# Layer 3's products in four tiles of 32 array columns

## The chip, the cores and the metric

One core of a Trainium2 chip runs the whole program. The metric is device time in microseconds for one execution; the median over runs is quoted. All runs below are of the fast state. Where two kernels are compared, the ratio is the mean time of one kernel's fast runs over the mean of the other's in the same rounds, so it is not quite the ratio of the medians quoted beside it.

## The reference, cut to what matters

Four graph-attention layers run over 16 batches of 1024 nodes with 256 features, in float32. The change touches layer 3, with 4 heads of 64 features:

```python
h = jnp.einsum('bnd,hde->bhne', nodes_embed, W)          # H = 4 heads, 64 features each
...
weight = jnp.where(node_adj[:, None] == 0, NEG, weight)
attention = jax.nn.softmax(weight, axis=-1)
dst = jnp.einsum('bhij,bhje->bhie', attention, h) + bias[None, :, None, :]
```

The kernel does not form the softmax. It makes unnormalized weights, and for each head multiplies them by 64 value columns and by one column whose product is the row's total. It divides afterwards.

## The kernel before

Two streams, one with the even batches and one with the odd, are traced side by side. Each generator yields its own cost in estimated microseconds, and `LAG` sets how far the second stream trails. A build-time scheduler then orders each engine's instructions. `tc.keep_in_program_order(x)`, called a pin below, adds one constraint: x comes after the instruction traced just before it on its engine. It does not forbid others in between.

VectorE makes a weight tile of 128 sources x 1024 destinations:

```python
for j in range(NI):                       # NI = 8 source blocks
    w = edges.tile([P, N], F32, name=f"weights{b % 2}")
    nc.vector.scalar_tensor_tensor(w, r, c(j), masks[b][:, j // 2, :, j % 2], op0=op, op1=ALU.mult)
    into.append(w)
    ...
    yield 0.5
```

Layer 3 then goes by head `h` and half `g` of the destinations:

```python
LAG = 120.0
...
for n in range(H * NH):                   # 4 heads x 2 halves
    h, g = divmod(n, NH)
    if g == NH - 1:
        behind = weigh3(h + 1)            # the next head's weights
        yield from start(behind, b)
    accT = accumulator(b)[: E + 1, :]     # 65 rows of one PSUM bank
    for j in range(NI):
        ...
        nc.tensor.matmul(accT, V3[:, j, h, :], weights[h * NI + j][:, ts(g, HALF)],
                         start=(j == 0), stop=(j == NI - 1))
        if n > 0:
            next(behind, None)
        yield 0.9
    ...
    sums = wide.tile([E + 1, HALF], F32, name="sums")
    nc.scalar.copy(sums, accT)
    next(coming, None)                    # a step of loading the batch after next
    ...
    for i in range(NG):
        nc.tensor.transpose(acc[:, i, :], sums[:, ts(i, P)], ident[: E + 1, : E + 1])
    inverse(inv, acc[:, :, E])
    nc.vector.tensor_mul(...)
```

The other layers' products are `nc.tensor.matmul(accs[i], weights[j][:, ts(i, P)], V[:, j, : D + 1], ...)`: 128 stationary columns (the operand that a weight load puts into TensorE's array first), 257 moving ones (streamed past it).

## Time and profile before

| | before |
|---|---|
| time, median of 4 runs | 3115.68 us (3114.26 to 3117.85) |
| span of the profiled run | 3112.0 us |
| TensorE busy | 2981.7 us (96%) |
| VectorE busy | 2337.8 us (75%) |
| layer-3 matmuls | 2048, of 65 stationary and 512 moving columns |

The page gives busy time by engine, then the chain of work that ended last, then groups of instructions by source line: output <- inputs, sizes, count | busy us, mean ns of one | idle time before and who ended it. The prediction below shows the lines that matter. A matmul's duration includes a tail that its neighbours hide, and the profile models a matmul's end rather than seeing it, so its price is read from the distance between starts, in the chain in order of time.

### The profile page before, as it was taken

How to read it: one execution, taken by the hardware profiler on the slowest of the kernel's cores; microseconds unless marked ns; L12 is line 12 of the kernel's file. 1: busy time of each engine (PE TensorE's matmuls, PEld its weight loads, DVE VectorE, ACT ScalarE, POOL GpSimd, SP SyncE). 2: the span in 40 equal slices, each digit the busy share in tenths (PEclk: the TensorE clock that was granted, in tenths of full speed). 3: DMA queues.
4: the chain of work that ended last, by engine and by line, in shares of the span. 5: the costliest groups of instructions: out<-in, count | busy, mean ns of one | idle time of the engine just before them, and what ended most of it. 6: DMA issues, size and time to landing. Idle time of an engine off the chain costs nothing.

```text
span 3112.0 us, 35525 instructions
## 1 busy us (share of the span) xinstructions
PE 2981.7 (96%) x12678; PEld 2047.5 (66%) x12678; DVE 2337.8 (75%) x5234; ACT 737.1 (24%) x1729; POOL 1081.2 (35%) x1405
## 2 busy tenths in 40 slices
PE   7899999999999999999999999999999999999986
PEld 5676756767566675766757667575666767667652
DVE  6678787777877768787786877778777787777856
ACT  1221312223131231312213122231322313122130
POOL 2323433244242333424244242342423434243332
PEclk9999999999999999999999999999999999999998
DMA  8112212022121122111122120221212222001010
GB/s 126 28 28 41 41 14 54 14 41 41 28 44 19 33 41 41 35 20 48 21 41 41 14 54 14 41 41 28 45 15 37 41 35 41 7 28 27 1 28 15
DMA packets 116872, 105.52 MB, mean 34 GB/s; under 512 B 73681, under 2 KB 91217, under 8 KB 116689
## 3 DMA queue, kind: packets, MB, share of 16 engines
q0 software_dynamic: 44256, 81.80, 16.2%
q1 hardware_dynamic: 72432, 21.37, 3.5%
q8 instruction: 103, 1.69, 0.2%
q14 instruction: 81, 0.66, 0.1%
HBM read 153.49 MB, written 33.55 MB: 60 GB/s over the span
## 4 chain that ended last, share of the span: by engine, by line
PE 78%; DVE 15%; POOL 3%; ACT 2%; issue 1%; DMA 1%; SPq 0%; ACTq 0%; POOLq 0%; DVEq 0%
PE acc L398 35%; PE acc L511 25%; PE acc L289 11%; DVE weights L310 8%; PE misc L282 3%; PE row L306 2%; ACT adj_i L141 1%; PE misc L526 1%; POOL y L471 1%; POOL rstd L257 1%; DVE V L355 1%; DVE stats L269 1%; POOL x_b L337 1%; DVE centered L274 1%; ACT below L333 1%
## 5 line engine op out<-in xcount | busy, mean ns | idle before, releaser
L398 PE MATMUL acc<-V,weights 128*128 128x257 f32 x6144 | 1449.3, 383 | 38.0 <-DVE weights L310 29.8
L398 PEld LDWEIGHTS acc<-V,weights 128*128 128x128 f32 x6144 | 1141.6, 190 | 348.6 <-DVE weights L310 100.6
L511 PE MATMUL acc<-weights,V 128*65 128x512 f32 x2048 | 955.9, 592 | 2.0 <-DVE weights L310 1.7
L310 DVE SCALAR_TENSOR_TENSOR weights<-row,ex,mask 128x1024 f32<-128x1024 f32 x512 | 627.8, 1274 | 6.1 <-PE row L306 5.6
L257 POOL TENSOR_TENSOR rstd<-rstd,minus_half 128x2 f32<-128x2 f32 (+1 forms) x320 | 299.5, 936 | 943.1 <-DVE rstd L256 930.7
L289 PE MATMUL acc<-W,hT 128*128 128x259 f32 (+1 forms) x2048 | 515.4, 389 | 26.0 <-ACT hT L284 14.8
L310 DVE SCALAR_TENSOR_TENSOR weights<-row,V,mask 128x1024 f32<-128x1024 f32 x384 | 482.0, 1274 | 46.6 <-PE row L306 46.6
L511 PEld LDWEIGHTS acc<-weights,V 128*65 128x65 f32 x2048 | 273.9, 138 | 361.0 <-issue 312.5
L289 PEld LDWEIGHTS acc<-W,hT 128*128 128x128 f32 x2048 | 379.2, 191 | 138.4 <-ACT hT L284 38.2
L337 POOL TENSOR_TENSOR x_b<-x_b,above 128x256 f32<-128x256 f32 x256 | 196.5, 771 | 427.5 <-DVE above L336 345.1
L333 ACT ACTIVATE below<-acc,inv 128x256 f32<-128x256 f32 x256 | 120.3, 473 | 771.4 <-DVE inv L326 623.6
L269 DVE BATCH_NORM_STATS2 stats<-x_b 128x6 f32<-128x256 f32 x512 | 207.6, 418 | 92.9 <-POOL x_b L337 83.5
L284 ACT COPY hT<-misc 128x512 f32<-128x512 f32 x256 | 146.7, 586 | 344.7 <-PE misc L282 344.6
L471 POOL TENSOR_TENSOR y<-y,bias 128x512 f32<-128x512 f32 x64 | 82.8, 1294 | 406.9 <-DVE y L529 323.5
L274 DVE TENSOR_SCALAR centered<-x_b,mv 128x256 f32<-128x256 f32 x512 | 192.6, 384 | 15.7 <-PE misc L282 12.2
L351 ACT ACTIVATE V<-acc,rstd 128x3 f32<-128x3 f32 x384 | 98.2, 262 | 418.0 <-PE acc L289 418.0
L282 PEld LDWEIGHTS misc<-ident,centered 128*128 128x128 f32 x1024 | 124.1, 141 | 109.7 <-issue 49.0
L282 PE MATMUL misc<-ident,centered 128*128 128x128 f32 x1024 | 162.7, 278 | 31.1 <-DVE centered L274 21.6
L335 DVE TENSOR_SCALAR above<-acc,inv 128x256 f32<-128x256 f32 x256 | 122.5, 481 | 84.4 <-ACT below L333 83.8
L521 ACT COPY sums<-acc 65x512 f32<-65x512 f32 x128 | 74.5, 582 | 409.6 <-PE acc L511 409.6
L355 DVE TENSOR_SCALAR V<-acc,rstd,V 128x256 f32<-128x256 f32 x256 | 133.4, 538 | 37.7 <-ACT V L351 34.9
L141 ACT ACTIVATE adj_i<-adj_i,minus_half 128x1024 bf16<-128x1024 bf16 x128 | 145.8, 1139 | 20.0 <-DMA adj_i<-in_adj_dram 20.0
(69 smaller groups left out, 1870.3 us busy)
## 6 DMA issues: line engine op xcount, KB each, us to landing
adj_i<-in_adj_dram POOLq DMA_DIRECT2D x128, 256.0 KB, 3.9
narrow<-in_adj_dram POOLq DMA_DIRECT2D x64, 256.0 KB, 9.4
out_dram<-y POOLq DMA_DIRECT2D x32, 512.0 KB, 4.3
x_b<-in_x_dram POOLq DMA_DIRECT2D x14, 1024.0 KB, 5.6
x_b<-in_x_dram SPq DMA_DIRECT2D x2, 1024.0 KB, 7.2
mask<-narrow SPq DMA_TRANSPOSE x64, 3.7
W<-in_L_gnn_W_dram SPq DMA_DIRECT2D x3, 256.0 KB, 6.1
weights<-in_L_gnn_a_dram SPq DMA_DIRECT2D x3, 256.0 KB, 7.9
```

The lines of the kernel that those rows point to most:

```text
L141: square = nc.scalar.activation(adj_i, adj_i, AF.Square, bias=minus_half, accum_out=squares[:, b, i : i + 1])
L257: nc.gpsimd.tensor_tensor(r, r, minus_half.to_broadcast([P, n]), op=ALU.pow)
L269: nc.vector.bn_stats(stats, xb[:, 2 * pair + n, :])
L274: nc.vector.tensor_scalar(centered[:, n, :], xb[:, 2 * pair + n, :], mv[:, n, 0:1], 0.0, op0=ALU.subtract, op1=ALU.max,)
L282: nc.tensor.transpose(turned[:, k, ts(n, P)], centered[:, n, ts(k, P)], ident)
L289: nc.tensor.matmul(projected, hT[:, k, ts(n, P)], W[l][:, k, :], start=(k == 0), stop=(k == NK - 1),)
L310: nc.vector.scalar_tensor_tensor(w, r, c(j), masks[b][:, j // 2, :, j % 2], op0=op, op1=ALU.mult)
L333: nc.scalar.activation(below, acc[:, :D], AF.Exp, scale=inv)
L337: nc.gpsimd.tensor_add(xi, xi, above)
L355: nc.vector.tensor_scalar(V[:, i, :D], projected[:, :D], rstd, V[:, i, D : D + 1], op0=ALU.mult, op1=ALU.mult,)
L398: nc.tensor.matmul(accs[i], weights[j][:, ts(i, P)], V[:, j, : D + 1], start=(j == 0), stop=(j == NI - 1),)
L511: nc.tensor.matmul(accT, V3[:, j, h, :], weights[h * NI + j][:, ts(g, HALF)], start=(j == 0), stop=(j == NI - 1),)
```

## The change

The intent is to fill the array. A product with 65 columns leaves about half of it empty. The changed kernel puts each product in a tile of 32 columns and issues four for four different tiles, to run side by side: two halves of the destinations x two halves of the 64 features. The totals get tiles of their own.

```diff
-    LAG = 120.0
+    LAG = 111.0
+    QUAD = P // 4
...
+        def in_tiles(parts, accT: bass.AP, first: bool, last: bool):
+            for n, (values, moving) in enumerate(parts):
+                made = nc.tensor.matmul(
+                    accT[ts(n, QUAD), :], values, moving, start=first, stop=last
+                )
+                if pinned:
+                    tc.keep_in_program_order(made)
+                pinned.append(made)
...
+        def add_values(h: int, j: int):
+            for n in (j + 1, j):
+                parts = [
+                    (V3[:, n, h, ts(e, QUAD)], moving)
+                    for moving in halves_of(h, n)
+                    for e in range(2)
+                ]
+                in_tiles(parts, acc, n == 1, n == NI - 2)
+
+        def add_totals(h: int, j: int):
+            parts = [
+                (V3[:, j + n, h, E:].to_broadcast([P, QUAD]), halves_of(h, j + n)[g])
+                for g, n in ((0, 1), (0, 0), (1, 1), (1, 0))
+            ]
+            in_tiles(parts, total, j == 0, j == NI - 2)
...
+        for h in range(H):
+            acc = accumulator(b)
+            total = accumulator(b)
+            if h == 0:
+                for j in range(0, NI, 2):
+                    next(behind)
+                    next(behind)
+                    pinned = []
+                    add_values(h, j)
+                    yield 1.8
...
+            step = 4 if h == 0 else 2
+            for first in range(0, NI, step):
+                pinned = []
+                for j in range(first, first + step, 2):
+                    add_totals(h, j)
+                    if h > 0:
+                        add_values(h, j)
+                for _ in range(step):
+                    next(behind, None)
+                yield 1.8 if h == 0 else 2.7
... (two copies of 128 x 512 a head, eight 128-column transposes, one reduction, one inverse,
     one multiply a head in place of two of half the size)
```

More of the change, by code (lines that the diff above doesn't have):

```diff
@@ L496, in weigh3, with halves_of @@
             )
+        def in_tiles(parts, accT: bass.AP, first: bool, last: bool):
[6 more added lines that the diff above has]
+                pinned.append(made)
+        def halves_of(h: int, j: int):
+            return [weights[h * NI + j][:, ts(g, HALF)] for g in range(NH)]
@@ L498, in batch @@
         behind = weigh3(0)
         yield from start(behind, b)
-        for n in range(H * NH):
-            h, g = divmod(n, NH)
-            if g == NH - 1:
-                behind = weigh3(h + 1)
-                yield from start(behind, b)
-            accT = accumulator(b)[: E + 1, :]
-            for j in range(NI):
-                if n == 0:
-                    next(behind)
-                nc.tensor.matmul(
-                    accT, V3[:, j, h, :], weights[h * NI + j][:, ts(g, HALF)],
-                    start=(j == 0), stop=(j == NI - 1),
-                )
-                if n > 0:
+        for h in range(H):
[3 more added lines that the diff above has]
+                for j in range(0, NI, 2):
+                    next(behind)
+                    next(behind)
+                    pinned = []
+                    add_values(h, j)
+                    yield 1.8
+                for _ in behind:
+                    pass
+            behind = weigh3(h + 1)
+            yield from start(behind, b)
+            step = 4 if h == 0 else 2
[6 more added lines that the diff above has]
+                for _ in range(step):
@@ L516, in batch @@
                     next(behind, None)
-                yield 0.9
+                yield 1.8 if h == 0 else 2.7
             for _ in behind:
                 pass
-            sums = wide.tile([E + 1, HALF], F32, name="sums")
-            nc.scalar.copy(sums, accT)
-            next(coming, None)
+            copies = []
+            for accT in (acc, total) if h == 0 else (total, acc):
+                copies.append(wide.tile([P, HALF], F32, name="sums"))
+                nc.scalar.copy(copies[-1], accT)
+                next(coming, None)
@@ L523, in batch @@
+            sums, totals = copies if h == 0 else copies[::-1]
             yield 0.5
-            acc = psum.tile([P, NG, E + 1], F32, name="misc")
+            turned = psum.tile([P, NG, P], F32, name="misc")
             for i in range(NG):
-                nc.tensor.transpose(acc[:, i, :], sums[:, ts(i, P)], ident[: E + 1, : E + 1])
-            inv = small.tile([P, NG], F32, name="inv4")
-            inverse(inv, acc[:, :, E])
+                nc.tensor.transpose(turned[:, i, :], totals[:, ts(i, P)], ident)
@@ L529, in batch @@
+            inv = small.tile([P, NH, NG], F32, name="inv8")
+            nc.vector.tensor_reduce(
+                inv, turned[:, :, ::QUAD].rearrange("p i (g n) -> p g i n", n=2), AX.X, ALU.add
+            )
+            inverse(inv, inv)
+            turned = psum.tile([P, NG, NH, E], F32, name="misc")
+            for i in range(NG):
+                nc.tensor.transpose(
+                    turned[:, i].rearrange("p g e -> p (g e)"), sums[:, ts(i, P)], ident
+                )
             nc.vector.tensor_mul(
-                y[:, ts(g, NG), h, :], acc[:, :, :E], inv.unsqueeze(2).to_broadcast([P, NG, E])
+                y[:, :, h, :].rearrange("p (g i) e -> p g i e", g=NH),
+                turned.rearrange("p i g e -> p g i e"),
+                inv.unsqueeze(3).to_broadcast([P, NH, NG, E]),
@@ L531, in batch @@
             )
             yield 0.5
-            if g == NH - 1:
-                if h > 0:
-                    rescale(*normed.pop())
-                normed.append(center(h))
-                yield 1.0
+            if h > 0:
+                rescale(*normed.pop())
+            normed.append(center(h))
+            yield 1.0
         for _ in coming:
```

## The prediction

> **What bounds the kernel now.** I read the page first: busy time by engine, the 40 slices, then the chain that ended last. These lines carry it:
>
> ```profile
> span 3112.0 us, 35525 instructions
> PE 2981.7 (96%) x12678; PEld 2047.5 (66%) x12678; DVE 2337.8 (75%) x5234; ACT 737.1 (24%) x1729; POOL 1081.2 (35%) x1405
> ...
> PE   7899999999999999999999999999999999999986
> ...
> PEclk9999999999999999999999999999999999999998
> ...
> PE 78%; DVE 15%; POOL 3%; ACT 2%; issue 1%; DMA 1%; SPq 0%; ACTq 0%; POOLq 0%; DVEq 0%
> ```
>
> TensorE is busy in nearly every slice at full clock and holds 78% of the chain. VectorE at 75% is second, with 15%. So a microsecond of matmul streaming removed is mostly a microsecond of the run, until VectorE's 2338 us become the floor. Next, the groups by line, for the one to be changed (layer 3's products) and those around it:
>
> ```profile
> L398 PE MATMUL acc<-V,weights 128*128 128x257 f32 x6144 | 1449.3, 383 | 38.0 <-DVE weights L310 29.8
> L511 PE MATMUL acc<-weights,V 128*65 128x512 f32 x2048 | 955.9, 592 | 2.0 <-DVE weights L310 1.7
> L511 PEld LDWEIGHTS acc<-weights,V 128*65 128x65 f32 x2048 | 273.9, 138 | 361.0 <-issue 312.5
> L521 ACT COPY sums<-acc 65x512 f32<-65x512 f32 x128 | 74.5, 582 | 409.6 <-PE acc L511 409.6
> L526 PE MATMUL misc<-ident,sums 65*128 65x65 f32 x512 | 55.9, 231 | 1.6 <-ACT sums L521 0.7
> L325 DVE TENSOR_SCALAR inv<-misc 128x4 f32<-128x4 f32 x128 | 19.4, 152 | 48.7 <-PE misc L526 48.6
> ```
>
> The program has 1024 layer-3 products (16 batches x 4 heads x 2 halves x 8 source blocks) and the trace has 2048 matmuls: each float32 product is two passes, each with its own weight load. Only 65 of 128 columns are used, while each pass streams all 512 moving columns. A duration is not the price: pipelined matmuls overlap their tails. The price is the distance between neighbours, from the timeline:
>
> ```profile
> 1539.43 0.87 PE acc L398 x4
> 1540.29 0.86 PE acc L511 x2
> 1541.15 2.60 PE acc L398 x12
> 1543.75 0.24 PE misc L526 x4
> 1543.99 0.88 PE row L306 x8
> 1544.87 2.57 PE acc L511 x6
> ```
>
> (That is the chain of waits in order of time: start, length, count.) Layer 3 costs 2.57/6 = 0.429 us a pass, 0.858 us a product. A 65-column transpose costs 0.24/4 = 0.06 us, a 128-column one 0.88/8 = 0.11 us. The two streams alternate every product or few. Layer 3 is 2048 x 0.429 = 879 us of TensorE, 28% of the span.
>
> **What the Trainium skill says.** (1) TensorEngine Tiling (Array Packing), section Key Properties: tiles can load and multiply in parallel, but changing the tiling mode drains the engine. No tiled product is in this trace, so it can neither confirm nor deny this. (2) TensorE: Matmul & The Clock Gate, section Measured speedup vs the span model: three column tiles of 32 with 512 columns gave 2.38 times, with some 4 ns more per tile. That need not be float32. (3) The same page, section The mechanism: matmuls start and end in strict program order. Under rivals I say why that matters for two passes. (4) The same page, section Single matmul latency: warm latency is (398 + N)/2.4 ns. The trace agrees if a float32 pass counts two cycles a column: (398 + 1024)/2.4 = 592.5 against 592 measured. So about 166 ns of a lone matmul are fill and drain, hidden among neighbours, and exposed at a drain.
>
> **The change part by part.**
>
> *Removed.* Of the 16 products per head (8 blocks x 2 halves, 65 columns) all go: 16 x 0.858 = 13.7 us a head, 879 us over 64 heads.
>
> *Added, values.* Per source block four products of 32 columns: two halves of the 512 destinations x two halves of the 64 features, one in each column tile. Eight groups of four a head.
>
> *Added, totals.* The 65th column becomes a 32-wide broadcast column. Two blocks and two halves fill the four tiles: one group of four per pair of blocks, four a head.
>
> If four tiles run side by side, a group of four costs what one product did, 0.858 us plus about 3 x 4 ns (the skill's figure). A head has 12 such groups where it had 16 products: 64 x 12 x 0.87 = 668 us. Saved: **211 us**. The author's own step costs say the same: 0.9 for a product before and 1.8 for two groups after.
>
> The instruction count triples: 768 groups x 4 x 2 = 6144 matmuls and as many loads. Can issue hold that? A group has 16 instructions in 0.86 us, 54 ns each. The transposes of 65 columns fit load and matmul in 60 ns, 30 each, so issue should not bind. Loads of 128 and 65 columns took 190 and 138 ns: 0.83 ns a column over 83 fixed, thus an estimated 110 ns for 32 columns. Eight of them are 0.88 us per group even if laid end to end, about the streaming time, so they are near the limit only if they cannot overlap one another.
>
> *Added, mode changes.* Holding a group in program order gives, per batch, 4 + 2 groups for head 0 and 4 for each other head: 18, or 288 in all. The other stream's 128-column work lies before and after nearly every one, so 576 changes. Each exposes at least the 0.166 us tail: 96 us. If the next weights cannot be loaded ahead across the change, add 0.11 us going in and 0.19 us coming out: 288 x 0.30 = 86 us, 182 together. Where two held groups meet, a change is saved. I take **120 us**.
>
> *Transposes.* Still eight a head, but of 128 columns: 512 x (0.11 - 0.06) = **+25 us** on TensorE.
>
> *VectorE and ScalarE.* The inverse is done once a head rather than twice (64 x 2 small operations at 152 to 172 ns fewer, 21 us), against 64 reductions of [128, 8, 2], perhaps 0.25 us each, 16 us. One multiply of 512 columns replaces two of 256. ScalarE still copies twice a head, 0.58 us each for 128 partitions instead of 65. All of this is about even, and beside the matmuls.
>
> *Moved.* Both accumulators of a stream are now held through a head, so the next head waits for a copy; the order of the copies is chosen to soften this. The other stream can fill the hole. LAG 120 to 111 only keeps the two streams half a (shorter) batch apart.
>
> Sum on TensorE: -211 + 25 + 120 = -66 us. 3116 - 66 is 3050. That the holds, copy order and lag look worked out makes me lean slightly to cheaper changes than I took (about 110): **3040 us**.
>
> **The rivals.** *First, strict order undoes the parallelism.* Tile 0's second pass must wait for its first. If a later matmul cannot start before it, tile 1's first pass overlaps only tile 0's second: two streams, not four. A group then costs four passes, 1.72 us, and layer 3 costs 768 x 1.72 = 1318 us, 439 more than now; the run would be near 3550 or beyond. For it: the strict-order statement above. Against it: tiles described as independent, and the kernel's step costs. I give it one in ten or a little more.
>
> *Second, the changes eat the gain.* At 182 us or more the sum is -4 us or a loss: 3100 to 3150. For it: fine alternation in the timeline, two single products between chunks of the other stream, and the very fact that the change needs to hold products together. Against it: larger groups of 8 to 12 products, 1.7 to 2.6 us each.
>
> *Third, VectorE becomes the bound.* It makes a head's weights in 8 x 1.274 = 10.2 us (the weights row has 1274 ns), and a head's matmuls fall from 13.7 to 10.4 us, so within a layer-3 stretch of one stream the engines draw level. Overall VectorE would be 2330/3040 = 77% busy, and the other stream's work lies between; I expect more waits for weights, some tens of microseconds at most. With free changes (96 us), -90 becomes about -60 on such waits. A hidden transfer is no rival: DMA is 1% of the chain.
>
> **Range and chances.** Full parallelism with the cheapest changes and a good mesh gives -150 (adjacent groups saving changes): 2960. Dear changes plus waits give +14 to +30: about 3140. Faster by over 2% means below 3054, and my centre lies just below that, with the long tail of the first rival above. Faster 0.55, within 2% 0.31, slower 0.14. The range for 8 in 10 is 2960 to 3140.
>
> **What would show it.** Parallel tiles: the layer-3 matmuls, now 6144 of them, keep durations near 592 ns but four start within a few tens of ns, and the stretch of one held set of 8 takes about 1.9 us rather than 3.4 (strict order). Mode changes: gaps or late starts of 0.17 to 0.35 us on TensorE at each border, by far most at borders of held groups. VectorE as the bound: its busy share above 80% and waits of TensorE for weights well above the 29.8 and 1.7 us of the rows above. Wrong altogether: matmul durations that grow with tiling, or weight loads that serialize, seen as weight-load busy near 100% in layer 3.

## The result, and the profile after

The changed kernel took **3066.68 us** (median of 4 runs, 3064.8 to 3068.5) against 3115.68. The ratio is 0.9842, 95% interval 0.9825 to 0.9859: 1.6% faster, which counts as within 2%. It lies inside the stated range and 27 us above the predicted 3040.

The page of the changed kernel, busy time by engine and the chain:

```profile
span 3063.2 us, 43637 instructions
PE 2934.9 (96%) x16774; PEld 1949.4 (64%) x16774; DVE 2341.3 (76%) x5106; ACT 737.8 (24%) x1729; POOL 1077.5 (35%) x1405
...
PE 78%; DVE 15%; POOL 3%; issue 1%; ACT 1%; DMA 1%; ACTq 0%; SPq 0%; POOLq 0%; DVEq 0%
```

TensorE still bounds the run with the same 78% of the chain, and the other engines' busy times barely move. The groups of the changed kernel (line numbers have shifted: L399 was L398, L502 was L511, L564 was L521):

```profile
L399 PE MATMUL acc<-V,weights 128*128 128x257 f32 x6144 | 1453.4, 386 | 41.3 <-DVE weights L311 24.0
...
L502 PE MATMUL acc<-weights,V 128*32 128x512 f32 x6144 | 780.0, 599 | 3.5 <-DVE weights L311 3.5
...
L502 PEld LDWEIGHTS acc<-weights,V 128*32 128x32 f32 x6144 | 171.2, 109 | 374.6 <-issue 371.1
...
L564 ACT COPY sums<-acc 128x512 f32<-128x512 f32 x128 | 75.1, 586 | 434.1 <-PE acc L502 433.0
```

There are three times as many layer-3 matmuls, each about as long as before (599 against 592 ns), yet together they are busy 780 instead of 956 us. So they do run side by side. A load of 32 columns takes 109 ns, and loads are not a bound. The transposes at the end of a head, from the groups with shapes kept apart:

```profile
L578 PE MATMUL misc<-ident,sums 128*128 128x128 f32 x256 | 39.4, 277 | 0.7 <-ACT sums L564 0.6
L570 PE MATMUL misc<-ident,sums 128*128 128x128 f32 x256 | 39.4, 276 | 0.7 <-ACT sums L564 0.7
```

Their busy time is 78.8 us where the 65-column ones had 55.9. The price of a tiled group, and of getting in and out of it, is in the chain in order of time (start, length, what):

```profile
1539.72 1.85 PE acc L502 x16
1541.57 1.06 PE acc L399 x4
1542.64 1.00 PE acc L502 x8
1543.63 1.06 PE acc L399 x4
1544.70 1.00 PE acc L502 x8
1545.69 1.06 PE acc L399 x4
```

Sixteen passes (two groups of four products) take 1.85 us and eight take 1.00. So one more group costs 0.85 us, as one product did before, and each unbroken run of tiled work costs 0.14 us on top. Four passes of 257 columns took 0.87 us in the kernel before (four times the 0.217 us of the 12 in 2.60 us) and take 1.06 here: 0.19 us more just after tiled work. An **excursion**, out of the 128-column mode and back, thus costs **0.33 us**.

Summing over each trace the distance from each matmul's start to the next one's, by kind of the first, gives a ledger of TensorE's time:

| us | before | after | change |
|---|---|---|---|
| layer-3 products | 889.5 | 755.0 | -134.5 |
| 257-column products of layers 0 to 2 | 1404.2 | 1420.9 | +16.7 |
| projections (259 and 268 columns) | 470.7 | 489.5 | +18.8 |
| transposes and weight rows | 315.7 | 365.0 | +49.3 |
| sum | | | -49.7 |

The spans differ by 48.8 us; the distances add up to nearly the span by construction, so the ledger shows only where the time went. Read by cause: with all groups full, streaming would fall from 879 to 768 groups x 0.857 = 658 us, -221. The trace has 382 unbroken runs of tiled matmuls, and 382 x 0.33 = +126. The wider transposes are 512 x 0.05 = +25.

That sums to -70, and it leaves out that **many groups are not full**. Some runs break a group, and a broken group costs as much as a full one: from its first start to the next other matmul, a run of one product took 0.976 us (median of 30), of three 0.990 (of 15), of four 0.996 (of 90), of seven 1.848, of eight 1.854. The same chain a little later shows runs of three, one, four and seven products (two passes each):

```profile
1552.94 0.99 PE acc L502 x6
...
1564.23 0.97 PE acc L502 x2
...
1566.22 1.00 PE acc L502 x8
...
1567.81 1.85 PE acc L502 x14
```

If each run of n products is counted as n/4 groups, rounded up, the 3072 products take 816 group times and not 768: 48 x 0.858 = +41. That brings the sum to -29. The remaining -20 is a fall in late starts and waits elsewhere (10 of it in layer 3's own 889.5 before, against 879) and was not taken apart; the time with no matmul in flight is about the same, 99 us before and 96 after.

### The profile page after: what moved, and what is told of

Same layout as the page of the kernel before. It is cut to its first block, busy times and chain, and to the rows that moved or that the text cites. A ratio compares the mean times of both kernels' runs of the same rounds, so it can differ in the third digit from the quotient of the medians.

```text
span 3063.2 us, 43637 instructions
## 1 busy us (share of the span) xinstructions
PE 2934.9 (96%) x16774; PEld 1949.4 (64%) x16774; DVE 2341.3 (76%) x5106; ACT 737.8 (24%) x1729; POOL 1077.5 (35%) x1405
## 4 chain that ended last, share of the span: by engine, by line
PE 78%; DVE 15%; POOL 3%; issue 1%; ACT 1%; DMA 1%; ACTq 0%; SPq 0%; POOLq 0%; DVEq 0%
PE acc L399 40%; PE acc L502 21%; PE acc L290 11%; DVE weights L311 6%; PE misc L283 3%; PE row L307 2%; DVE stats L270 1%; DVE centered L275 1%; POOL x_b L338 1%; DVE V L356 1%; POOL rstd L258 1%; DVE above L336 1%; POOL y L486 1%; DVE y L485 1%; ACT below L334 1%
## 5 line engine op out<-in xcount | busy, mean ns | idle before, releaser
L399 PE MATMUL acc<-V,weights 128*128 128x257 f32 x6144 | 1453.4, 386 | 41.3 <-DVE weights L311 24.0
L399 PEld LDWEIGHTS acc<-V,weights 128*128 128x128 f32 x6144 | 1131.2, 190 | 374.0 <-DVE weights L311 87.7
L502 PE MATMUL acc<-weights,V 128*32 128x512 f32 x6144 | 780.0, 599 | 3.5 <-DVE weights L311 3.5
L290 PE MATMUL acc<-W,hT 128*128 128x259 f32 (+1 forms) x2048 | 523.2, 392 | 28.1 <-ACT hT L285 16.7
L502 PEld LDWEIGHTS acc<-weights,V 128*32 128x32 f32 x6144 | 171.2, 109 | 374.6 <-issue 371.1
L338 POOL TENSOR_TENSOR x_b<-x_b,above 128x256 f32<-128x256 f32 x256 | 188.0, 737 | 467.9 <-DVE above L337 431.5
L326 DVE TENSOR_SCALAR inv<-acc 128x1 f32<-128x1 f32 x256 | 37.4, 150 | 194.2 <-PE acc L399 192.8
L564 ACT COPY sums<-acc 128x512 f32<-128x512 f32 x128 | 75.1, 586 | 434.1 <-PE acc L502 433.0
```

Of the source, the lines that this page charges most:

```text
L290: nc.tensor.matmul(projected, hT[:, k, ts(n, P)], W[l][:, k, :], start=(k == 0), stop=(k == NK - 1),)
L338: nc.gpsimd.tensor_add(xi, xi, above)
L502: made = nc.tensor.matmul(accT[ts(n, QUAD), :], values, moving, start=first, stop=last)
```

## The experiments

Theory A: the gain is limited by the price of excursions, so fewer excursions are faster. Theory B: the excursions are where the other stream fills waits, so taking them away gives waits. Theory C: tiles do not run side by side when the program lists two products for one tile in a row. Theory D: the late starts at a group's borders come from operands, not from the mode. A fifth question is what the lag did.

**One variant needed no run.** Without any pin (`if pinned: tc.keep_in_program_order(made)` deleted) the build gives the same order of instructions on all five engines. As written, holding the products in program order does nothing: the scheduler already kept this order, and a pin keeps nobody out. In the build the 382 runs are far from the planned groups of 8 and 12 products: 30 are a single product and 90 are four. The cuts fall behind the first product of a group: the 30 single ones are all for tile 0, and 153 runs begin with tile 1.

### e1: pin the first product of a group too

```diff
-                if pinned:
-                    tc.keep_in_program_order(made)
+                tc.keep_in_program_order(made)
```

Now each group follows what its own program order traced before it, and the runs have 8, 12 or more products.

> The first product of a held group is pinned too; in the build the layer-3 products then form 245 unbroken runs on TensorE instead of 382 (128-column work never falls inside a group). Theory A (what limits the gain is the price of each excursion into the 32-column mode, read from the trace of the changed kernel as 0.33 us: 0.14 going in, 0.19 coming out): 137 fewer excursions x 0.33 = 45 us less, near 3021 us. Theory B (the interruptions filled waits for weights, so removing them only turns them into waits): no gain, 3055 to 3080, with waits of TensorE on VectorE's weights up by about as much as the excursions saved.

Measured: 3139.34 us (3138.21 to 3142.13), ratio to before 1.0076 (1.0063 to 1.0090). It has 245 excursions, and is 73 us slower than the changed kernel. TensorE's timeline (start, length, what, and in brackets the idle time before):

```profile
1569.82 0.60 PE L569 MATMUL misc<-ident,sums 128*128 128x128 f32 x4
1570.25 0.60 PE L577 MATMUL misc<-ident,sums 128*128 128x128 f32 x4
1574.46 1.09 PE L307 MATMUL row<-ident,V 128*128 128x128 f32 x8 [3.61 <-DVE weights L311]
1577.86 2.86 PE L399 MATMUL acc<-V,weights 128*128 128x257 f32 x5 [2.31 <-DVE weights L311]
```

TensorE has run out of work that is ready and waits for VectorE's weights, 3.6 us and again 2.3. Over the whole run the waits of TensorE in e1 are

```profile
PE acc L399 <- DVE weights L311: 79.5, 65, 2.3
PE row L307 <- DVE weights L311: 61.2, 17, 5.3
```

(us in total, times, longest), where the changed kernel has only

```profile
PE acc L399 <- DVE weights L311: 24.0, 19, 2.1
```

Time without any matmul in flight, summed over the traces, rose from 96 to 201 us, +105. A second loss follows the waits: the mean clock granted to TensorE was 0.976 in e1's profiled run, against 0.993 in the changed kernel. Fifteen times, 191 us apart, a wait of 3.6 us is followed, about 1 us after its end, by 6.8 us at half clock, in which the passes of 257 columns start 0.428 us apart and not 0.217. The stretch after the wait shown above (its window and length, then busy time and count of PE, PEld, DVE, ACT and POOL, the granted clock, and DMA):

```profile
1575.00:1582.00 7.00, 4.69 (x15) 2.95 (x13) 6.66 (x12) 0.00 (x0) 1.26 (x1) 0.53 0.00 0
```

Matmuls were in flight at half clock for 92 us in e1 and for 16 in the changed kernel (the end of the run left out). Half of the difference, 38 us, is my estimate of what that cost.

On the other side, 137 excursions x 0.33 = 45 us are saved, and another 41 because no group is broken in e1 (768 group times). 105 + 38 - 86 = 57 of the 73 us. Theory A's premise, the price, survives; its conclusion falls. Theory B has the direction right: holding tighter loses more in waits than it saves. Its range, 3055 to 3080, is missed: the waits rose by more than twice the 45 us. Open: e1, e2 and e3 ran at lag 111 alone, and e8 to e11 show that the lag by itself moves the changed kernel by 68 us. Whether tighter groups would win at another lag was not tested.

### e2: e1 with four source blocks to a group

```diff
-            step = 4 if h == 0 else 2
+            step = 4
...
-                yield 1.8 if h == 0 else 2.7
+                yield 1.8 if h == 0 else 5.4
```

(and the pin of e1)

> As the run with the first product pinned, and the heads after the first take four source blocks to a group instead of two: 185 runs instead of 382. Theory A (price per excursion 0.33 us): 197 x 0.33 = 65 us less than the changed kernel, near 3002. Theory B (larger held groups wait for weights): no better than the run with 245 excursions, or worse, with longer waits of TensorE on weights at the start of groups.

Measured: 3203.97 us (3202.09 to 3205.26), ratio 1.0283 (1.0269 to 1.0297). It has the fewest excursions of all, 185, and is the slowest; time without a matmul in flight is 238 us, and matmuls were in flight at half clock for 139 us. Theory B's direction again.

### e3: four source blocks to a group, pins as in the change

The edit is that of e2 without the pin of e1.

> Four source blocks to a group after the first head, pins as in the changed kernel: 337 runs instead of 382. Theory A: 45 x 0.33 = 15 us less, near 3052. Theory B: same as the changed kernel, 3067, or slower.

Measured: 3106.07 us (3104.12 to 3109.54), ratio 0.9972 (0.9961 to 0.9983); 337 excursions. It is 39 us slower than the changed kernel although 45 excursions fewer should have saved 15. Coarser steps alone undo most of the gain. The trace shows some of why: 121 us without a matmul in flight (+25), and 47 us of matmul at half clock against 16 (an estimated +15). But TensorE's largest wait here is for VectorE's centered nodes (42.6 us), not for the weights that theory B names (12.3 us).

### e4: the same tile twice in a row

```diff
-            for n in (j + 1, j):
-                parts = [ ... for moving in halves_of(h, n) for e in range(2) ]
-                in_tiles(parts, acc, n == 1, n == NI - 2)
+            for g in range(NH):
+                for e in range(2):
+                    for n in (j + 1, j):
+                        made = nc.tensor.matmul(
+                            acc[ts(2 * g + e, QUAD), :], V3[:, n, h, ts(e, QUAD)],
+                            halves_of(h, n)[g], start=(n == 1), stop=(n == NI - 2),
+                        )
+                        ...  # pinned as before
```

> The eight value products of a pair of blocks are issued tile by tile (tile 0 twice, tile 1 twice, ...) instead of tile 0, 1, 2, 3 and again. Nearly the same number of runs (383). Theory A (each column tile has its own queue within a window, matmuls of different tiles start when their tile is free): the same as the changed kernel, 3067 within 20. Theory C (strict program order for all matmuls, so a later tile may not start before an earlier tile's last pass has begun): eight products are 16 passes of which only 3 overlap, 13 x 0.43 = 5.6 us in place of 1.7 for each of 256 pairs, about 1000 us slower, near 4060.

Measured: 3086.65 us (3083.12 to 3089.14), ratio 0.9904 (0.9889 to 0.9920); 383 excursions. This is 20 us over the changed kernel, not 1000. The chain of e4 in order of time (L518 are the values, L502 the totals):

```profile
1548.05 0.99 PE acc L502 x8
1549.05 1.75 PE acc L518 x16
1550.80 0.86 PE acc L502 x8
```

Sixteen passes of values, listed two products to a tile, take 1.75 us; in the order of the change they take 1.71 (the 1.85 above less the 0.14 of going in). Their records start in fours within 60 ns. Theory C asked for 5.6 us and falls: a product for tile 1 does not wait for the two listed before it for tile 0. What is not shown is who lets it pass, the engine or the order in which the passes are emitted; the trace does not name a pass's tile. Where the 20 us come from can be read from the runs: 61 are single products against 30, and counted as above the products take 847 group times against 816, 31 x 0.858 = 27 us more. Time with no matmul in flight is 8 us less (88 against 96).

### e5 and e6: excursions of no use, and their control

To the kernel before, 288 one-column products are added in the middle of the other layers' work, writing to PSUM columns of the same bank that nobody reads (`spare`). In e5 they are 32 columns wide, in e6 65.

```diff
                 if i > 1:
                     for j in range(NI):
                         product(i, j)
+                        if j == NI // 2 - 1:
+                            nc.tensor.matmul(
+                                spare[i][:32, :1], V[:, j, :32], weights[j][:, :1],   # e6: 65 for 32
+                                start=False, stop=False, skip_group_check=True,
+                            )
```

> The kernel before, with 288 one-column products added in the middle of the other layers' unbroken 128-column work (six per layer and batch, layers 0 to 2), each 32 columns wide and so in the 32-column mode, written to columns that nobody reads: 288 excursions of no use. Theory A (an excursion costs 0.33 us of TensorE whoever makes it): 288 x 0.33 = 95 us plus the products' own two short passes, slower than the kernel before by 95 to 130 us, and slower than the control of 65 columns by 70 to 110. Theory D (the late starts seen at the borders of the groups come from waiting operands, not from the mode): no more than the control, within 15 us of it.

> The control: the same 288 added products at the same places, 65 columns wide like the layer-3 products of the kernel before, so without a change of mode. Both theories: two passes of one column and two loads of 65 columns, some 0.05 to 0.2 us each, 15 to 55 us slower than the kernel before.

Measured: e5 3200.24 us (3198.02 to 3201.63), ratio 1.0274 (1.0260 to 1.0288). e6 3151.76 us (3148.7 to 3154.24), ratio 1.0119 (1.0104 to 1.0135). Both have the same order on TensorE. Per added product e5 costs (3200.24 - 3114.4)/288 = 0.30 us over the kernel before in the same rounds, and e6 (3151.76 - 3114.4)/288 = 0.13. The chains in order of time, e5 first (L425 is the added product):

```profile
1511.82 0.65 PE acc L400 x3
1512.47 0.15 PE acc L425 x2
1512.63 3.66 PE acc L400 x16
```

```profile
1510.79 0.87 PE acc L400 x4
1511.66 0.06 PE acc L425 x2
1511.72 3.57 PE acc L400 x16
```

Sixteen passes of 257 columns cost 16 x 0.217 = 3.47 us, so the useless product costs 0.15 + 0.19 = 0.34 us in the 32-column mode and 0.06 + 0.10 = 0.16 without a change of mode. Theory D falls: it allowed 15 us between the two runs, and 48.5 were measured (3200.24 - 3151.76). So a change of mode has a price with nothing to wait for, about 0.17 us for going in and out. Theory A's ranges were missed as well, both from below: e5 is 86 us over the kernel before, not 95 to 130, and 48 over the control, not 70 to 110. Half of the 0.34 is paid by a one-column product without any change of mode, so that it is close to the 0.33 of the changed kernel is partly chance. There the products are long, and 65-column products of the same length cost their neighbours nothing in the kernel before (two in 0.86 us, then twelve passes of 257 columns at 0.217 each, in the prediction's view). The whole 0.33 thus comes with the tiles; how much of it is the mode, and how much the first loads of four tiles, was not separated.

### e7 to e11: the lag

e7 is the kernel before with `LAG = 111.0`; e8, e10 and e11 are the changed kernel with 120, 114 and 108. e9 is e8 with the nodes of the batch after next fetched earlier:

```diff
             tc.keep_in_program_order(turn)
+            if b > 1 and c == 1:
+                fetch_nodes(b)
             yield
         if b > 1:
-            fetch_nodes(b)
             yield
```

> The kernel before with the changed kernel's lag between the two streams and nothing else. If the lag alone carried part of the gain, this is faster than 3116; I expect it within 10 us of 3116, as the lag only follows half the shortened batch.

> The changed kernel with the old lag; 346 runs of layer-3 products in the build instead of 382. By the price of an excursion alone 36 x 0.33 = 12 us faster, 3055; if how the two streams mesh matters more (as the run with the first product pinned showed), it lies anywhere from 3055 to 3110, and slower is likelier because the lag was chosen with the change.

> The changed kernel with the old lag (3135 us), and the next batch's nodes fetched some steps earlier; the order on TensorE, with 346 runs, stays. If the loss of 68 us against lag 111 is the wait of VectorE for those nodes at each batch's start (63 us in 14 waits in the trace, 5 us with lag 111), this comes to 3075 to 3090. If the two streams mesh worse on the engines and the wait is only a symptom, it stays at 3120 to 3140.

> The changed kernel with lag 114: 341 runs. The price of excursions alone gives 41 x 0.30 = 12 us faster than lag 111, 3054; if the mesh of the streams decides, anything between 3060 and 3135, and a smooth slope between 111 and 120 would give 3090.

> The changed kernel with lag 108, half a batch exactly by the kernel's own step costs: 375 runs. If the lag was tuned and its optimum is narrow, 3070 to 3110; if it matters only above 111, within 10 us of 3067.

| run | kernel | lag | us (lowest to highest) | ratio to before | 95% |
|---|---|---|---|---|---|
| e7 | before | 111 | 3119.59 (3114.94 to 3123.13) | 1.0016 | 1.0009 to 1.0022 |
| e8 | after | 120 | 3135.03 (3128.01 to 3142.41) | 1.0064 | 1.0050 to 1.0078 |
| e9 | after, early fetch | 120 | 3104.10 (3099.99 to 3107.36) | 0.9963 | 0.9951 to 0.9975 |
| e10 | after | 114 | 3134.54 (3133.79 to 3144.88) | 1.0071 | 1.0056 to 1.0087 |
| e11 | after | 108 | 3058.66 (3058.09 to 3059.51) | 0.9819 | 0.9804 to 0.9834 |

The kernel before hardly cares whether the lag is 120 or 111. The changed kernel depends on it: with the old lag the tiles would have been a **loss** of 0.6%. There is no slope: 108 and 111 are alike, 114 and 120 are alike, and some 68 us lie between. e8's page and its waits:

```profile
PE 62%; DVE 24%; POOL 6%; DMA 5%; ACT 2%; issue 1%; ACTq 0%; SPq 0%; POOLq 0%; DVEq 0%
```

```profile
DVE stats L270 <- DMA x_b<-in_x_dram: 63.3, 14, 8.4
```

and e9's:

```profile
PE 68%; DVE 22%; POOL 5%; ACT 2%; issue 1%; DMA 1%; ACTq 0%; SPq 0%; POOLq 0%; DVEq 0%
```

```profile
DVE stats L271 <- DMA x_b<-in_x_dram: 5.3, 1, 5.3
```

With the long lag a batch starts before its nodes have landed, 14 times. The early fetch removes that wait and returns 31 of the 68 us. So the late fetch is one cause, measured. The other 37 us lie largely in more time without a matmul in flight (123 us in e9 against 96) and in matmuls at half clock (49 us in flight against 16, an estimated 17 us), less the 12 us of 36 excursions saved. Why the streams mesh worse, with VectorE still at 22% of the chain instead of 15%, remains open. e11 is the fastest kernel run, 8 us below the changed one by the medians, but the two ratios come from different rounds and their intervals overlap, so it is no clear gain.

### e12: head 0 like the others

```diff
-                for j in range(0, NI, 2):
-                    next(behind)
-                    next(behind)
-                    pinned = []
-                    add_values(h, j)
-                    yield 1.8
+                for j in range(NI):
+                    next(behind)
+                    yield 0.9
...  (and step = 2 with values and totals together for every head)
```

> The changed kernel with head 0 treated like the other heads: all its eight weights are made first, its values are multiplied together with its totals while head 1's weights are made. Four groups for head 0 instead of six, but 384 runs in the build (382 before), so no gain from excursions. If having work for TensorE while weights are being made is what counts, it is slower: per batch 8 x 1.27 = 10 us in which this stream gives TensorE nothing; at most 16 x 10 / 2 = 80 us, less what the other stream fills: 3080 to 3140. If the single groups of four between the other stream's products are what costs, faster, 3040 to 3060.

Measured: 3065.82 us (3064.67 to 3066.84), ratio 0.9842 (0.9827 to 0.9857): the same as the change, with 384 excursions. Neither of the two expectations came true. How head 0 is started does not matter to the time. By the trace two effects nearly cancel: more broken groups (845 group times against 816, 25 us), and less time without a matmul in flight (80 us against 96). That the other stream covers the missing work is only argued.

## Why the prediction was right or wrong

*What bounds the kernel* was right: TensorE kept 78% of the chain, and the ledger of its starts has its change in TensorE's work.

*Parallel tiles* were right: a full group of four was predicted at 0.87 us and measured at 0.857. Four products in four tiles cost what one did. The first rival, which leaned on the Trainium skill ("TensorE: Matmul & The Clock Gate", section The mechanism: strict order of matmuls), fell in the trace and again in e4.

*Loads and issue* were right: 109 ns a load against the estimated 110, and no bound. The check of 592.5 against 592 ns is none, though: the profile models where a matmul ends.

*Transposes* were right: their starts lie 0.109 us apart, and lay 0.062 apart before. *VectorE* stayed even (2337.8 to 2341.3 us), so the third rival did not come about in the changed kernel; e1 shows long waits for its weights all the same, at a busy share of still 75%.

*Mode changes* were sized at 120 us for 288 excursions at 0.17 to 0.32 us a change, that is 0.33 to 0.63 an excursion. Measured: 382 excursions at 0.33, 126 us. The sum was right by luck, because two errors cancelled: I took the held groups as unbroken (94 excursions too few, 31 us), and the price lay at the cheap end. It equals the bare tail of 2 x 0.166 us, but that it is this tail is not shown. That a change of mode costs anything, which the trace before could not show, is as the Trainium skill says ("TensorEngine Tiling (Array Packing)", section Key Properties).

*The step that failed* is "A head has 12 such groups" together with "Holding a group in program order gives ... 288 in all": full groups that nothing breaks. The hold does nothing at all, the groups are broken, and 3072 products take 816 group times, so streaming falls by 180 us and not by 211. Against this error of 31 us, and 6 more for the mode changes, stands a fall of 20 us in other late starts and waits that the sum did not hold. So the worked sum of -66 came within 17 us of the measured -49 partly by luck. The last lean, "slightly to cheaper changes than I took (about 110)", had no support in the runs and took the number 10 us further off: the predicted 3040 was 27 us too low, and the likelier class on record, faster by over 2%, did not come.

*A second step, that the lag only keeps the spacing, was wrong without showing in the time*: "LAG 120 to 111 only keeps the two streams half a (shorter) batch apart". e8 shows that it decides the sign of the result. Nothing in the working would have found that; it came out right because the diff brought a good lag along.

## What to carry to other kernels

Column tiles gave their full factor here even with two-pass float32, but only where all four were issued together: a group with one product cost as much as one with four. Each trip into the tiled mode and back cost about a third of a microsecond of TensorE. Count the trips and the broken groups in the built order, not in the source. Be wary of buying fewer trips with blocks that nothing may interrupt: in e1, e2 and e3, all at one lag, fewer trips were slower each time, as TensorE waited more, and part of the work after the waits ran at half clock. And when work is taken out of one of two interleaved streams, rerun the offset between them on both sides of the change, as a good cut with the old offset can measure as a loss.

## What the Trainium skill lacked or had wrong

- "TensorEngine Tiling (Array Packing)", section Key Properties, names the drain at a change of mode without a size. Here: 0.14 us going in and 0.19 coming out around long tiled products, and 0.34 us for a useless trip of two one-column passes, of which 0.16 are also paid by a 65-column product without a change of mode.
- "TensorE: Matmul & The Clock Gate", section The mechanism, has matmuls in strict order. Here products listed twice for one tile in a row still ran four abreast: 16 passes in 1.75 us instead of the 5.6 us that strict order of the passes asks for (with the reserve named at e4: the passes may have been emitted in another order than listed, so this does not show the page wrong).
- The same page, section Measured speedup vs the span model, gives 2.38 times for three column tiles and no figure for four. In a steady stream of float32, four tiles gave 0.858 x 4 / 0.857 = 4.0 times.
- "FP8 and Floating Point Precision", section TensorE Precision Notes, gives float32 as four passes through the array. The trace shows them as two matmuls per product, each with its own weight load, 0.429 us apart for 512 columns and 0.217 for 257, so some 0.83 ns a column. That the page does not say.
